# One image's convolution shared between VectorE and TensorE: diagonal taps, a norm by products, and a new pace for the image ahead

## The chip, the cores and the metric

The kernel runs on one core of a Trainium2 chip. Its time is given in device microseconds (us); a figure for a kernel is the median of several executions. One further execution is taken with the hardware profiler, and all rows of the profile come from that one.

## The reference

The input `x` holds 16 images of 56 × 56 tokens with 384 channels, in float32. Two layers follow each other, both with a residual and a group norm of 32 groups (12 channels each) ahead:

```python
# layer 0: windowed attention (windows of 7 x 7, 12 heads of 32, shifted by 3)
x = x + _L0_conv_ref(_gn(x), w_qkv, w_out, b_out, rel_pos_table)
# layer 1: depthwise convolution, 3 x 3, one filter per channel
x = x + _L1_conv_ref(_gn(x), L1_conv_w)

def _gn(v, G=32, eps=1e-5):
    g = v.reshape(B_, H_, W_, G, C_ // G)
    m = jnp.mean(g, axis=(1, 2, 4), keepdims=True)
    s = jnp.var(g, axis=(1, 2, 4), keepdims=True)
    return ((g - m) / jnp.sqrt(s + eps)).reshape(v.shape)

def _L1_conv_ref(x, w):
    w_clip = jnp.clip(w, -1.0, 1.0)
    binary_kernel = w_clip + lax.stop_gradient(jnp.sign(w_clip) - w_clip)
    k = binary_kernel.reshape(kh, kw, 1, C * mult)
    return lax.conv_general_dilated(x, k, ..., padding='SAME', feature_group_count=C)
```

The convolution's weights are the signs of the clipped `w`. The second norm's sums run over a whole image, so no band of an image can be convolved before the attention of its last window is done.

## The kernel before, in words

Channels lie on the partitions: three chunks (`NC`) of 128 channels. The attention works in stripes of 7 rows (8 per image, 128 in all), and each stripe in two units of 4 windows, so there are 256 units, 16 (`NU`) per image. `all_units` walks the units and writes out the order by hand: `heavy(u)` gives the products of a unit (`value`, `query_key`, `project`), and between them stand scores (L458), softmax (L475), exponential (L493), the sums by key (`add_up`, L529), the inverse (L567 to L570, ScalarE and then VectorE), `attend` (L549) and `divide` (L577). `project` (L588) adds the residual on VectorE (L596), takes the second norm's statistics (L602), and sends the stripe through POOL's queue into `mid`, a DRAM tile with the wrap-around columns repeated (L608 to L613).

The convolution of an image runs beside the attention of the next one. `plan_conv` gives each of its steps a due time in units (`at(when, f, ...)`), and `all_units` starts a step when its time comes; the program order on each engine is the order in which the steps are started, and each engine and each DMA queue takes them in that order. An image has 12 pieces: 4 bands (`NB`) of 14 rows (`BR`), each with 3 chunks. For a piece, `band` loads 16 rows from `mid` through SP's queue into one of two buffers `xb` (L636); `pad` has ScalarE write the normalized rows into `hp`, a frame of 16 × 58 with zeros around, of which there are two (L651); `middle` has ScalarE write residual and center tap into `acc` (L663, with the factors that `center` prepared); `tap` has VectorE add the other eight taps, one instruction each (L676). When the three chunks of a band are done, `store` has TensorE transpose them, 112 tokens at a time, into PSUM banks (L687), ScalarE copies them out (L688), and SP stores them (L692), two tiles per store with three buffers. PSUM has four banks for all this (`bank`), taken in turn.

The norm ahead of it is `norm_gather` (means and variances per channel, L244 and L246; then by DMA through DRAM to one group per partition, L248 and L250) and `norm_scale` (folds over the 12 channels of a group on POOL, the power, and by DMA through DRAM back to channels, L285 and L287).

All images have `step` 1.3 units per piece; image 14, which runs beside the attention of image 15, has 1.1, so that its last steps fall behind unit 255:

```python
plan_conv(b - 1, NU * b, 1.3 if b < B - 1 else 1.1, 3, 0.6, nc.gpsimd)
```

Image 15 has no attention to run beside. Its plan has step 1.0 and starts at unit 256; what is left of image 14's plan is sorted in by the due times, and all is started in that order:

```python
plan_conv(B - 1, B * NU, 1.0, 1.3, 0.1, nc.sync)
for _, g, a in sorted((i for u in side for i in side[u]), key=lambda i: i[0]):
    g(*a)
```

After it come a few small steps that test whether a softmax overflowed (L846 to L855); if so, a slower path runs again, which doesn't happen with these inputs. The input `gmat` holds, for each pair of chunks that share a group, a 128 × 128 matrix with 1/12 where two channels are of one group; the kernel before doesn't read it.

Of the kernel before, what the change touches and what calls it, by code (L numbers as in the profile page):

```python
# [9 lines left out]
F32 = mybir.dt.float32  # L10
I32 = mybir.dt.int32
AF = mybir.ActivationFunctionType
# [3 lines left out]
WIN = 7  # L16
SHIFT = WIN // 2
GROUPS = 32
EPS = 1e-5
# [15 lines left out]
def kernel(  # L35
# [57 lines left out]
    def bank(name):  # L93
        return ps.tile([P, 512], F32, tag="mm", name=name)
# [7 lines left out]

    least = const.tile([P, 1], F32, tag="least", name="least")
    reach = const.tile([P, 2, B * NU], F32, tag="reach", name="reach")
    seen = const.tile([P, B], F32, tag="seen", name="seen")
    again = const.tile([P, 1], I32, tag="again", name="again")
    wq_t = const.tile([P, NC, 3 * C], F32, tag="wq", name="wq_t")
    wo_t = const.tile([P, NC, C], F32, tag="wo", name="wo_t")
# [144 lines left out]
    def norm_scale(key, queue, pool=nc.gpsimd):  # L253

        gt = parts.pop(key)
        name = "%d_%d" % key
        g = small.tile([GROUPS, 4], F32, tag="g", name=f"g{name}")
        mean, var, rstd, shift = (g[:, n : n + 1] for n in range(4))
        if key[0]:
            var = seen[:GROUPS, key[1] : key[1] + 1]  # L260
        dev = small.tile([GROUPS, GS], F32, tag="dev", name=f"dev{name}")

        def fold(x):

            n = GS
            while n > 1:
                half = n // 2
                pool.tensor_tensor(x[:, :half], x[:, :half], x[:, n - half : n], ALU.add)
                n -= half

        pool.tensor_copy(dev, gt[:, :, 0])
        fold(dev)
        pool.tensor_scalar(mean, dev[:, 0:1], 1.0 / GS, None, ALU.mult)
        pool.tensor_tensor(dev, gt[:, :, 0], mean.to_broadcast([GROUPS, GS]), ALU.subtract)
        pool.tensor_tensor(dev, dev, dev, ALU.mult)
        pool.tensor_tensor(dev, dev, gt[:, :, 1], ALU.add)
        fold(dev)
        pool.tensor_scalar(var, dev[:, 0:1], 1.0 / GS, EPS, ALU.mult, ALU.add)
        nc.gpsimd.tensor_tensor(rstd, var, power[:GROUPS], ALU.pow)
        pool.tensor_tensor(shift, mean, rstd, ALU.mult)  # L280
        pool.tensor_scalar(shift, shift, -1.0, None, ALU.mult)
        both = small.tile([GROUPS, GS, 2], F32, tag="both", name=f"both{name}")
        pool.tensor_copy(both, g[:, 2:4].unsqueeze(1).to_broadcast([GROUPS, GS, 2]))
        by_channel = dram.tile([C, 2], F32, tag="cod", name=f"cod{name}")
        queue.dma_start(by_channel.rearrange("(g n) k -> g (n k)", n=GS), both.rearrange("g n k -> g (n k)"))  # L285
        coef = small.tile([P, NC, 2], F32, tag="coef", name=f"coef{name}", bufs=4)
        queue.dma_start(coef, by_channel.rearrange("(c p) k -> p c k", p=P))  # L287
        coefs[key] = coef

# [287 lines left out]
    def project(s, m):  # L579

        b, r = divmod(s, NS)
        if (1, b) not in stats:
            stats[1, b] = small.tile([P, NC, NS, 6], F32, tag="st1", name=f"st1_{b}", bufs=1)
        if m == 0:
            ys[s] = ypool.tile([P, NC, WIN, R], F32, tag="y", name=f"y_{s}")
        py = bank(f"py_{s}_{m}")
        for c in range(NC):
            nc.tensor.matmul(  # L588
                py[:, :ST],
                wo_t[:, c, m * P : (m + 1) * P],  # L590
                ots[s][:, c, :],
                start=(c == 0),
                stop=(c == NC - 1),
            )
        view = ys[s][:, m, :, SHIFT:R]
        nc.vector.tensor_tensor(  # L596
            view.rearrange("p r (w c) -> p w r c", c=WIN),
            py[:, :ST].rearrange("p (w r c) -> p w r c", r=WIN, c=WIN),
            xs[s][:, m, :].rearrange("p (w r c) -> p w r c", r=WIN, c=WIN),
            ALU.add,  # L600
        )
        nc.vector.bn_stats(stats[1, b][:, m, r, :], view)  # L602
        if m == NC - 1:
            if b not in mids:
                mids[b] = dram.tile([P, NC, H, R], F32, tag="mid", name=f"mid_{b}")
            del xs[s]
            yt = ys.pop(s)
            nc.gpsimd.tensor_copy(yt[:, :, :, 0:SHIFT], yt[:, :, :, W:R])  # L608
            r0 = r * WIN + SHIFT
            n = min(WIN, H - r0)  # L610
            nc.gpsimd.dma_start(mids[b][:, :, r0 : r0 + n, :], yt[:, :, 0:n, :])
            if n < WIN:
                nc.gpsimd.dma_start(mids[b][:, :, 0 : WIN - n, :], yt[:, :, n:WIN, :])  # L613


    mids, bands, outs, centers = {}, {}, {}, {}

    def center(b):

        coef = coefs[1, b]  # L620
        pool = nc.gpsimd
        cen = small.tile([P, NC, 2], F32, tag="cen", name=f"cen_{b}")
        pool.tensor_tensor(cen[:, :, 0], coef[:, :, 0], bo_sb, ALU.mult)
        pool.tensor_tensor(coef[:, :, 1], coef[:, :, 1], cen[:, :, 0], ALU.add)
# [13 lines left out]

    count, padded = [0], {}

    def pad(b, k, c):

        coef, cen = coefs[1, b], centers[b]
        xb, rows, at, n = bands.pop((b, k, c))
        hp = hps[count[0] % 2]
        count[0] += 1
        if k == 0:
            nc.gpsimd.memset(hp[:, 0, :], 0.0)
        if k == NB - 1:
# [7 lines left out]
        )  # L657
        padded[b, k, c] = (hp, xb)

    def middle(b, k, c):  # L660
        hp, xb = padded[b, k, c]
        acc = opool.tile([P, BR, W], F32, tag="o", name=f"o_{b}_{k}_{c}")
        nc.scalar.activation(  # L663
            acc,
            xb[:, 1 : BR + 1, 0:W],
            AF.Identity,
            bias=centers[b][:, c, 1:2],
            scale=centers[b][:, c, 0:1],
        )
        outs[b, k, c] = acc  # L670
# [6 lines left out]
            acc, hp[:, dy : dy + BR, dx : dx + W], dw_t[:, c, t : t + 1], acc, ALU.mult, ALU.add  # L677
        )

    def store(b, k, g):  # L680
        todo = range(g * LG, min((g + 1) * LG, BR * W // OT))
        flat = [outs[b, k, c].rearrange("p h w -> p (h w)") for c in range(NC)]
        xo = io.tile([P, LG, C], F32, tag="io", name=f"xo_{b}_{k}_{g}")
        for n, t in enumerate(todo):
            po = bank(f"px_{b}_{k}_{t}")
            for c in range(NC):
                nc.tensor.transpose(po[:OT, c * P : (c + 1) * P], flat[c][:, t * OT : (t + 1) * OT], ident)  # L687
            nc.scalar.copy(xo[:OT, n, :], po[:OT, :C])  # L688
        n = len(todo)
        first = k * BR * W + g * LG * OT  # L690
        rows = out[b].rearrange("h w c -> (h w) c")[first : first + n * OT, :]
        nc.sync.dma_start(rows.rearrange("(t p) c -> p t c", p=OT), xo[:OT, :n])  # L692


    side = {}
# [64 lines left out]
    def plan(last_queue):  # L760
        for b in range(1, B):
            plan_load(b)
            plan_conv(b - 1, NU * b, 1.3 if b < B - 1 else 1.1, 3, 0.6, nc.gpsimd)

    def all_units(fast):
        for m in range(2 * NC):
# [12 lines left out]
        for u in range(B * NU):  # L779
# [25 lines left out]
                    g(*a)  # L805
            for _, g, a in light:
                g(*a)
        plan_conv(B - 1, B * NU, 1.0, 1.3, 0.1, nc.sync)
        for _, g, a in sorted((i for u in side for i in side[u]), key=lambda i: i[0]):
            g(*a)  # L810
        side.clear()
# [2 lines left out]
    with tc.manual_schedule():  # L814
# [30 lines left out]
        for n in range(2):  # L845
            nc.vector.tensor_scalar(reach[:, n], reach[:, n], MOST[n], None, ALU.is_lt)  # L846
        nc.vector.tensor_reduce(worst[:, 0:1], reach.rearrange("p n u -> p (n u)"), AX.X, ALU.min)
        fine = small.tile([P, B], F32, tag="fine", name="fine")
        nc.vector.tensor_scalar(fine, seen, 1.0e37, None, ALU.is_lt)
        nc.vector.tensor_reduce(worst[:, 1:2], fine, AX.X, ALU.min)  # L850
        pf = bank("pf")
# [69 lines left out]
```

## Time and profile before

| | us |
|---|---|
| Median of 3 runs | 4300.38 (4299.23 to 4300.46) |
| The profiled execution | 4298.77 |
| Its span, first to last instruction | 4297.0 |
| TensorE busy over the span | 4125.1 (96%) |
| VectorE | 3478.0 (81%) |
| ScalarE | 2479.2 (58%) |
| GpSimd (POOL) | 1800.4 (42%) |
| Granted TensorE clock, mean | 0.980 |

A row of the timeline reads: start in us from the span's start, duration, engine and line, operation, out<-in by the program's names, shapes, how many instructions were merged into the row; in brackets how long the engine had been idle and whose step ended that. PE is TensorE's matmuls, PEld its weight loads, DVE VectorE, ACT ScalarE, SPq the DMA issues of SP's queue. A float32 product shows as two matmuls and two weight loads, a transpose as one of each.

The attention's last product ends at about 4158 us; some 139 us of the span come after it.

### The profile page before, as it was taken

What the parts mean: (1) busy time and instruction counts of PE and PEld (TensorE: products, weight loads), DVE (VectorE), ACT (ScalarE), POOL (GpSimd) and SP (SyncE); (2) the same over time, 40 slices, a digit from 0 to 9 for tenths busy, and PEclk for the clock granted to TensorE, in tenths of its full rate; (3) what the DMA queues carried; (4) which work ended last, traced back from release to release, by engine and by line L of the source; (5) the groups of instructions that cost most, each with busy time, mean ns of one, the idle gap of its engine ahead of it and who ended that gap; (6) DMA issues with size and microseconds to landing.
All of it is one profiled execution on the core that took longest, in us unless ns stands there. A gap on an engine that the chain in (4) does not pass through costs nothing.

```text
span 4297.0 us, 155602 instructions
## 1 busy us (share of the span) xinstructions
PE 4125.1 (96%) x68041; PEld 2628.4 (61%) x68041; DVE 3478.0 (81%) x4387; ACT 2479.2 (58%) x5269; POOL 1800.4 (42%) x3182
## 2 busy tenths in 40 slices
PE   5999999999999999999999999999999999999961
PEld 3666666666666666666666666666666666666641
DVE  4546879788887888888788887878888788887878
ACT  2545656566565656656565665656656565665542
POOL 4453545254443534535345454535444353441000
PEclk8999999999999999999999999999999999999985
DMA  4434445454444544445454444545444454443332
GB/s 90 79 66 82 109 103 123 101 110 110 108 101 109 117 103 114 109 101 112 99 118 107 108 106 104 122 101 109 107 111 100 109 117 102 115 101 87 97 84 88
DMA packets 997170, 444.81 MB, mean 104 GB/s; under 512 B 877690, under 2 KB 935067, under 8 KB 996482
## 3 DMA queue, kind: packets, MB, share of 16 engines
q1 hardware_dynamic: 906480, 272.64, 30.0%
q0 software_dynamic: 87824, 159.76, 15.1%
q8 instruction: 538, 8.81, 0.9%
q10 hardware_dynamic: 2178, 2.38, 0.2%
q14 instruction: 150, 1.23, 0.1%
HBM read 174.86 MB, written 158.47 MB: 78 GB/s over the span
## 4 chain that ended last, share of the span: by engine, by line
PE 94%; DVE 3%; DMA 1%; issue 1%; ACT 0%; SPq 0%; POOL 0%; ACTq 0%; DVEq 0%; POOLq 0%
PE pq L404 36%; PE pv L417 18%; PE py L588 18%; PE ps L458 7%; PE po L549 7%; PE ps L529 4%; PE px L687 3%; DVE o L676 2%; SPq L440 0%; DMA xl<-in_x_dram 0%; DMA wl<-in_L_conv_w_out_dram 0%; DMA xn<-in_x_dram 0%; DMA out_dram<-xo 0%; DMA vq<-in_x_dram 0%; DMA e<-in_x_dram 0%
## 5 line engine op out<-in xcount | busy, mean ns | idle before, releaser
L404 PE MATMUL pq<-xn,wq_t 128*128 128x392 f32 x4608 | 1591.4, 497 | 0.0
L676 DVE SCALAR_TENSOR_TENSOR o<-hp,dw_t,o 128x784 f32<-128x784 f32 x1536 | 1559.4, 1020 | 31.8 <-ACT o L663 17.7
L351 POOL DMA_DIRECT2D xl<-in_x_dram x1980 | 1328.8, 724 | 179.7 <-DVE xt L368 105.1
L404 PEld LDWEIGHTS pq<-xn,wq_t 128*128 128x128 f32 x4608 | 844.6, 188 | 586.8 <-issue 2.6
L588 PE MATMUL py<-ot,wo_t 128*128 128x392 f32 x2304 | 820.2, 498 | 3.9 <-DVE ot L577 3.9
L417 PE MATMUL pv<-xn,wq_t 128*128 128x392 f32 x2304 | 816.8, 496 | 1.3 <-ACT xn L393 1.3
L411 ACT COPY qk<-pq 128x392 f32<-128x392 f32 x768 | 371.4, 484 | 704.6 <-PE pq L404 701.0
L569 DVE SCALAR_TENSOR_TENSOR ln<-ps,inv 128x588 f32<-128x588 f32 x256 | 197.0, 769 | 540.2 <-ACT inv L568 536.5
L608 POOL COPY y<-y 128x63 f32<-128x63 f32 x128 | 33.5, 262 | 1392.3 <-DVE y L596 1392.2
L417 PEld LDWEIGHTS pv<-xn,wq_t 128*128 128x128 f32 x2304 | 420.3, 188 | 284.6 <-ACT xn L393 2.4
L588 PEld LDWEIGHTS py<-ot,wo_t 128*128 128x128 f32 x2304 | 421.5, 190 | 274.4 <-DVE ot L577 4.1
L424 ACT COPY vt<-pv 128x392 f32<-128x392 f32 x384 | 189.2, 493 | 450.7 <-PE pv L417 449.7
L493 ACT ACTIVATE e<-e 128x1176 f32<-128x1176 f32 x256 | 303.1, 1184 | 234.2 <-DVE e L475 234.2
L458 PEld LDWEIGHTS ps<-qk 32*64 32x64 f32 x24576 | 308.5, 131 | 144.5 <-issue 106.0
L549 PE MATMUL po<-e,v 49*32 49x49 f32 x24576 | 363.1, 212 | 8.2 <-DMA v<-vq 7.5
L475 DVE SCALAR_TENSOR_TENSOR e<-ps,bias 128x1176 f32<-128x1176 f32 x256 | 349.2, 1364 | 26.3 <-PE ps L458 24.3
L549 PEld LDWEIGHTS po<-e,v 49*32 49x32 f32 x24576 | 354.1, 105 | 13.9 <-issue 8.8
L458 PE MATMUL ps<-qk 32*64 32x49 f32 x24576 | 340.9, 225 | 1.5 <-issue 1.2
L687 PE MATMUL px<-ident,o 128*112 128x128 f32 x1344 | 202.7, 286 | 103.7 <-DVE o L676 89.7
L380 ACT COPY x<-xt 128x196 f32<-128x196 f32 x720 | 225.8, 369 | 93.8 <-DVE xt L368 92.6
L428 DVE STREAM_TRANSPOSE vq<-vt 128x512 f32<-128x512 f32 x384 | 267.6, 698 | 5.9 <-ACT vt L424 5.7
L688 ACT COPY xo<-px 112x384 f32<-112x384 f32 x448 | 195.1, 482 | 123.7 <-PE px L687 94.1
(120 smaller groups left out, 3653.6 us busy)
## 6 DMA issues: line engine op xcount, KB each, us to landing
v<-vq SPq DMA_DIRECT2D x2048, 48.0 KB
mid<-y POOLq DMA_DIRECT2D x112, 619.5 KB
xl<-in_x_dram POOLq DMA_DIRECT2D x1260, 52.5 KB
out_dram<-xo SPq DMA_DIRECT2D x192, 336.0 KB
xb<-mid SPq DMA_DIRECT2D x96, 472.0 KB
xb<-mid SPq DMA_DIRECT2D x96, 442.5 KB
out_dram<-xo SPq DMA_DIRECT2D x64, 168.0 KB
mid<-y POOLq DMA_DIRECT2D x16, 354.0 KB
```

The lines of the kernel that those rows point to most:

```text
L351: nc.gpsimd.dma_start(xz[i * D + lo : i * D + hi, c, k : k + n, :], flat[token : token + n * (hi - lo)].rearrange("(k t) c -> t k c", k=n) ...
L404: nc.tensor.matmul(pq[:, :ST].rearrange("p (w t) -> p w t", t=T), wq_t[:, c, m * P : (m + 1) * P], xn[:, c, :, :T], start=(c == 0), stop=( ...
L411: nc.scalar.copy(qk[:, m, :ST], pq[:, :ST])
L417: nc.tensor.matmul(pv[:, :ST].rearrange("p (w t) -> p w t", t=T), wq_t[:, c, 2 * C + m * P : 2 * C + (m + 1) * P], xn[:, c, :, :T], start= ...
L428: nc.vector.transpose(vq[:, :, :, m].rearrange("p h n d -> p n h d"), vt[:, m].rearrange("p (n w) (j b) -> p n (w j) b", w=2, b=D),)
L458: nc.tensor.matmul(pp[row * HT : (row + 1) * HT, i, k0 : k0 + T], qk[part, NC * fast + j, q0 : q0 + HT], qk[part, NC * (not fast) + j, q0 ...
L475: nc.vector.scalar_tensor_tensor(e, pp[:, :, : NC * 2 * T].rearrange("q i (n k) -> q i n k", k=T), QSCALE, bias[:, int(s % NS == NS - 1)]. ...
L493: nc.scalar.activation(flat, flat, AF.Exp, accum_out=reach[:, 0, u : u + 1])
L549: nc.tensor.matmul(po[w][i * D : (i + 1) * D, (2 * j + r) * T : (2 * j + r + 1) * T], vs[s][keys, n * 2 + r, h * D : (h + 1) * D], by_head ...
L588: nc.tensor.matmul(py[:, :ST], wo_t[:, c, m * P : (m + 1) * P], ots[s][:, c, :], start=(c == 0), stop=(c == NC - 1),)
L676: nc.vector.scalar_tensor_tensor(acc, hp[:, dy : dy + BR, dx : dx + W], dw_t[:, c, t : t + 1], acc, ALU.mult, ALU.add)
L687: nc.tensor.transpose(po[:OT, c * P : (c + 1) * P], flat[c][:, t * OT : (t + 1) * OT], ident)
```

## The change

Four things are done for the last image, and one for the image ahead of it.

- The norm of image 15 (`norm_late`): the group sums are two sets of seven products with `gmat` instead of DMAs through DRAM and folds on POOL; the power stays on POOL, and `center` runs on VectorE.
- The third chunk of each band (c = 2) of image 15: `convolve` makes its eight outer taps by TensorE, with `hp` as weights (114 columns: two rows of 56 tokens and the two between) and a diagonal matrix per tap as the moving operand; the ninth product adds `acc` by the identity. The result comes out by token, so it needs no transpose; `carry` copies it from PSUM to SBUF (ScalarE) and stores it (SP, two DMAs per band). The other two chunks keep their taps on VectorE, and `store` takes two chunks.
- What this needs is prepared at units 250 to 253.4 (`fetch_late`, `diagonal`), in buffers of the pool that held the stripes' inputs.
- `plan_last` gives all steps of image 15 their due times. `mid`'s last two writes go through SP's queue instead of POOL's.
- Image 14's pace is 0.95 units per piece instead of 1.1.

The diff, without two hunks that only widen the tiles `seen` and `fine` from B to B + NC columns:

```diff
@@ -286,6 +286,66 @@
         coef = small.tile([P, NC, 2], F32, tag="coef", name=f"coef{name}", bufs=4)
         queue.dma_start(coef, by_channel.rearrange("(c p) k -> p c k", p=P))
         coefs[key] = coef
+    late_tiles = {}
+    def fetch_late():
+        pairs = group_blocks(C, GS)
+        gm = xpool.tile([P, NC, ST], F32, tag="x", name="gm").rearrange("p c n -> p (c n)")[:, : len(pairs) * P]
+        gm = gm.rearrange("p (n q) -> p n q", q=P)
+        nc.sync.dma_start(gm, gmat)
+        dg = xpool.tile([P, NC, ST], F32, tag="x", name="dg").rearrange("p c n -> p (c n)")[:, : 9 * P]
+        dg = dg.rearrange("p (t q) -> p t q", q=P)
+        hp = xpool.tile([P, NC, ST], F32, tag="x", name="hp_late").rearrange("p c n -> p (c n)")
+        hp = hp[:, : (BR + 2) * (W + 2)].rearrange("p (h w) -> p h w", w=W + 2)
+        acc = xpool.tile([P, NC, ST], F32, tag="x", name="acc_late").rearrange("p c n -> p (c n)")
+        acc = acc[:, : BR * (W + 2)].rearrange("p (h w) -> p h w", w=W + 2)
+        for t in (hp, acc):
+            nc.gpsimd.memset(t, 0.0)
+        late_tiles.update(gm=gm, dg=dg, hp=hp, acc=acc)
+    def diagonal(t):
+        nc.scalar.activation(late_tiles["dg"][:, t], ident, AF.Identity, scale=dw_t[:, NC - 1, t : t + 1])
+    def norm_late(b):
+        st, gm = stats.pop((1, b)), late_tiles["gm"]
+        mv = small.tile([P, NC, 2], F32, tag="mv", name="mv_late")
+        for c in range(NC):
+            nc.vector.bn_aggr(mv[:, c, :], st[:, c].rearrange("p s k -> p (s k)"))
+        nc.vector.tensor_tensor(mv[:, :, 0], mv[:, :, 0], bo_sb, ALU.add)
+        def group_mean(x, name):
+            pg = bank(name)
+            pairs = group_blocks(C, GS)
+            for m in range(NC):
+                of_m = [n for n, (k, j) in enumerate(pairs) if j == m]
+                for n in of_m:
+                    k = pairs[n][0]
+                    nc.tensor.matmul(
+                        pg[:, 4 * m : 4 * m + 1],
+                        gm[:, n, :],
+                        x[:, k : k + 1],
+                        start=(n == of_m[0]),
+                        stop=(n == of_m[-1]),
+                    )
+            return pg[:, : 4 * NC].rearrange("p (m f) -> p m f", f=4)[:, :, 0]
+        mean = group_mean(mv[:, :, 0], "pg_mean")
+        dev = small.tile([P, 3, NC], F32, tag="dev_late", name="dev_late", bufs=1)
+        nc.vector.tensor_copy(dev[:, 2], mean)
+        nc.vector.tensor_tensor(dev[:, 0], mv[:, :, 0], dev[:, 2], ALU.subtract)
+        nc.vector.tensor_tensor(dev[:, 0], dev[:, 0], dev[:, 0], ALU.mult)
+        nc.vector.tensor_tensor(dev[:, 0], dev[:, 0], mv[:, :, 1], ALU.add)
+        var = seen[:, B : B + NC]
+        nc.vector.tensor_scalar(var, group_mean(dev[:, 0], "pg_var"), EPS, None, ALU.add)
+        nc.gpsimd.tensor_tensor(dev[:, 1], var, power.to_broadcast([P, NC]), ALU.pow)
+        coef = small.tile([P, NC, 2], F32, tag="coef", name="coef_late", bufs=4)
+        nc.vector.tensor_copy(coef[:, :, 0], dev[:, 1])
+        nc.vector.scalar_tensor_tensor(coef[:, :, 1], dev[:, 2], -1.0, dev[:, 1], ALU.mult, ALU.mult)
+        coefs[1, b] = coef
...
@@ -608,17 +668,17 @@
             nc.gpsimd.tensor_copy(yt[:, :, :, 0:SHIFT], yt[:, :, :, W:R])
             r0 = r * WIN + SHIFT
             n = min(WIN, H - r0)
-            nc.gpsimd.dma_start(mids[b][:, :, r0 : r0 + n, :], yt[:, :, 0:n, :])
+            queue = nc.sync if s == B * NS - 1 else nc.gpsimd
+            queue.dma_start(mids[b][:, :, r0 : r0 + n, :], yt[:, :, 0:n, :])
             if n < WIN:
-                nc.gpsimd.dma_start(mids[b][:, :, 0 : WIN - n, :], yt[:, :, n:WIN, :])
+                queue.dma_start(mids[b][:, :, 0 : WIN - n, :], yt[:, :, n:WIN, :])
     mids, bands, outs, centers = {}, {}, {}, {}
-    def center(b):
+    def center(b, pool=nc.gpsimd):
         coef = coefs[1, b]
-        pool = nc.gpsimd
         cen = small.tile([P, NC, 2], F32, tag="cen", name=f"cen_{b}")
         pool.tensor_tensor(cen[:, :, 0], coef[:, :, 0], bo_sb, ALU.mult)
         pool.tensor_tensor(coef[:, :, 1], coef[:, :, 1], cen[:, :, 0], ALU.add)
...
@@ -638,12 +698,12 @@
     count, padded = [0], {}
-    def pad(b, k, c):
+    def pad(b, k, c, late=False):
         coef, cen = coefs[1, b], centers[b]
         xb, rows, at, n = bands.pop((b, k, c))
-        hp = hps[count[0] % 2]
-        count[0] += 1
+        hp = late_tiles["hp"] if late else hps[count[0] % 2]
+        count[0] += not late
         if k == 0:
             nc.gpsimd.memset(hp[:, 0, :], 0.0)
         if k == NB - 1:
...
@@ -657,11 +717,11 @@
         )
         padded[b, k, c] = (hp, xb)
-    def middle(b, k, c):
+    def middle(b, k, c, late=False):
         hp, xb = padded[b, k, c]
-        acc = opool.tile([P, BR, W], F32, tag="o", name=f"o_{b}_{k}_{c}")
+        acc = late_tiles["acc"] if late else opool.tile([P, BR, W], F32, tag="o", name=f"o_{b}_{k}_{c}")
         nc.scalar.activation(
-            acc,
+            acc[:, :, :W],
             xb[:, 1 : BR + 1, 0:W],
             AF.Identity,
             bias=centers[b][:, c, 1:2],
...
@@ -677,19 +737,81 @@
             acc, hp[:, dy : dy + BR, dx : dx + W], dw_t[:, c, t : t + 1], acc, ALU.mult, ALU.add
         )
-    def store(b, k, g):
+    def store(b, k, g, chunks=NC):
         todo = range(g * LG, min((g + 1) * LG, BR * W // OT))
-        flat = [outs[b, k, c].rearrange("p h w -> p (h w)") for c in range(NC)]
+        flat = [outs[b, k, c].rearrange("p h w -> p (h w)") for c in range(chunks)]
         xo = io.tile([P, LG, C], F32, tag="io", name=f"xo_{b}_{k}_{g}")
         for n, t in enumerate(todo):
             po = bank(f"px_{b}_{k}_{t}")
-            for c in range(NC):
+            for c in range(chunks):
                 nc.tensor.transpose(po[:OT, c * P : (c + 1) * P], flat[c][:, t * OT : (t + 1) * OT], ident)
-            nc.scalar.copy(xo[:OT, n, :], po[:OT, :C])
+            nc.scalar.copy(xo[:OT, n, : chunks * P], po[:OT, : chunks * P])
         n = len(todo)
         first = k * BR * W + g * LG * OT
-        rows = out[b].rearrange("h w c -> (h w) c")[first : first + n * OT, :]
-        nc.sync.dma_start(rows.rearrange("(t p) c -> p t c", p=OT), xo[:OT, :n])
+        rows = out[b].rearrange("h w c -> (h w) c")[first : first + n * OT, : chunks * P]
+        nc.sync.dma_start(rows.rearrange("(t p) c -> p t c", p=OT), xo[:OT, :n, : chunks * P])
+    summed = {}
+    def convolve(b, k, c):
+        hp, _ = padded[b, k, c]
+        pitch = W + 2
+        both = pitch + W
+        hp, acc = (a.rearrange("p h w -> p (h w)") for a in (hp, outs[b, k, c]))
+        tiles = BR * W // OT
+        summed[k] = []
+        for first in range(0, tiles, 4):
+            n = min(4, tiles - first)
+            pc = bank(f"pc_{k}_{first}")
+            summed[k].append((first, n, pc))
+            for i in range(n):
+                here = pc[:both, i * P : (i + 1) * P]
+                row = 2 * (first + i)
+                for t in (0, 1, 2, 3, 5, 6, 7, 8):
+                    dy, dx = divmod(t, 3)
+                    nc.tensor.matmul(
+                        here,
+                        hp[:, (row + dy) * pitch + dx : (row + dy) * pitch + dx + both],
+                        late_tiles["dg"][:, t],
+                        start=(t == 0),
+                        stop=False,
+                    )
+                nc.tensor.matmul(here, acc[:, row * pitch : row * pitch + both], ident, start=False, stop=True)
+    def carry(b, k, c):
+        by_token = xpool.tile([P, NC, ST], F32, tag="x", name=f"xc_{k}").rearrange("p c n -> p (c n)")
+        tiles = BR * W // OT
+        both = 2 * W + 2
+        for first, n, pc in summed.pop(k):
+            nc.scalar.copy(by_token[:both, first * P : (first + n) * P], pc[:both, : n * P])
+        rows = out[b].rearrange("h w c -> (h w) c")[k * BR * W : (k + 1) * BR * W, c * P : (c + 1) * P]
+        for j in range(2):
+            nc.sync.dma_start(
+                rows.rearrange("(t j p) c -> j p t c", j=2, p=W)[j],
+                by_token[j * (W + 2) : j * (W + 2) + W, : tiles * P].rearrange("p (t c) -> p t c", c=P),
+            )
+    def plan_last(b, first):
+        at(first, norm_late, b)
+        at(first + 0.1, center, b, nc.vector)
+        for k in range(NB):
+            for c in (2, 0, 1):
+                n = 2 * k + c
+                when = first + 0.5 + (2 * k if c == 2 else n)
+                at(when - (0.1 if c == 2 else 0.2), band, b, k, c)
+                at(when - (0.05 if c == 2 else 0.15), pad, b, k, c, c == 2)
+                at(when - (0.04 if c == 2 else 0.14), middle, b, k, c, c == 2)
+                if c == 2:
+                    at(when + 0.2, convolve, b, k, c)
+                    at(when + 1.3, carry, b, k, c)
+                    continue
+                for i, t in enumerate((0, 1, 2, 3, 5, 6, 7, 8)):
+                    at(when + i / 8, tap, b, k, c, t)
+            for g in range(-(-BR * W // OT // LG)):
+                at(first + 0.5 + 2 * k + 2.02 + 0.01 * g, store, b, k, g, NC - 1)
     side = {}
...
@@ -760,7 +882,10 @@
     def plan(last_queue):
         for b in range(1, B):
             plan_load(b)
-            plan_conv(b - 1, NU * b, 1.3 if b < B - 1 else 1.1, 3, 0.6, nc.gpsimd)
+            plan_conv(b - 1, NU * b, 1.3 if b < B - 1 else 0.95, 3, 0.6, nc.gpsimd)
+        at(B * NU - 6, fetch_late)
+        for t in range(9):
+            at(B * NU - 5 + 0.3 * t, diagonal, t)
     def all_units(fast):
         for m in range(2 * NC):
...
@@ -805,7 +930,7 @@
                     g(*a)
             for _, g, a in light:
                 g(*a)
-        plan_conv(B - 1, B * NU, 1.0, 1.3, 0.1, nc.sync)
+        plan_last(B - 1, B * NU)
         for _, g, a in sorted((i for u in side for i in side[u]), key=lambda i: i[0]):
             g(*a)
         side.clear()
```

## The prediction

> **What bounds the kernel now.** I read the chain that ended last first, limited to the last 167 us, because the diff touches only image 14's convolution (its pace) and everything of image 15 after its attention:
>
> ```profile
> by line: DVE o L676 60.0%; issue 10.0%; PE py L588 4.1%; DMA mvd<-mv 2.3%; DMA out_dram<-xo 1.6%; DMA gt<-mvd 1.6%; DMA coef<-cod 1.2%; ACT xo L688 1.1%; PE px L687 1.1%; DVE st L602 1.0%; POOL dev L268 0.9%; DVE ln L570 0.9%; DVE ln L569 0
> ```
>
> Before this stretch TensorE is busy without a gap; here VectorE's taps (L676) carry the end. The timeline gives the three stages I price: last unit, norm, convolution.
>
> ```profile
> 4141.00 1.38 DVE L475 SCALAR_TENSOR_TENSOR e<-ps,bias 128x1176 f32<-128x1176 f32 x1
> 4142.29 5.37 DVE L676 SCALAR_TENSOR_TENSOR o<-hp,dw_t,o 128x784 f32<-128x784 f32 x5
> 4143.59 1.03 ACT L663 ACTIVATE o<-xb,cen 128x784 f32<-128x784 f32 x1
> ...
> 4147.58 0.76 DVE L569 SCALAR_TENSOR_TENSOR ln<-ps,inv 128x588 f32<-128x588 f32 x1
> ...
> 4161.52 0.82 DVE L244 BATCH_NORM_AGGREGATE mv<-st 128x2 f32<-128x48 f32 x3
> ...
> 4178.31 1.09 ACT L651 ACTIVATE hp<-xb,coef 128x840 f32<-128x840 f32 x1 [31.07 <-POOL coef L624]
> ...
> 4181.19 101.59 DVE L676 SCALAR_TENSOR_TENSOR o<-hp,dw_t,o 128x784 f32<-128x784 f32 x96 [17.71 <-ACT o L663]
> ```
>
> Image 14's taps stand between the last softmax and the last product; from the statistics' end (4161.52) to the first padded band (4178.31) 16.8 us pass; then 96 taps run in 101.59 us, 1.058 each, nearly without a gap. Two more things matter, TensorE's transposes at both clocks and how long a band takes to come:
>
> ```profile
> 4124.33 0.82 PE L687 MATMUL px<-ident,o 128*112 128x128 f32 x6
> 4206.66 4.30 PE L687 MATMUL px<-ident,o 128*112 128x128 f32 x19 [7.98 <-DVE o L676]
> 4261.12 0.41 SPq L636 DMA_DIRECT2D xb<-mid  x1
> 4266.41 1.09 ACT L651 ACTIVATE hp<-xb,coef 128x840 f32<-128x840 f32 x1 [3.69 <-DMA xb<-mid]
> ```
>
> In the trace the first six start 108 ns apart (clock 1.00), the nineteen 213 ns apart (clock 0.50). A band costs 4.2 us (4187.56 to 4191.72) to 5.3 us (these rows) from issue to pad. The table of TensorE's clock by window:
>
> ```profile
> 4147.40:4150.80 3.40, 0.72 (x1) 0.50 0.00 0
> 4150.80:4154.20 3.40, 3.40 (x7) 0.50 0.00 0
> 4154.20:4157.70 3.50, 3.50 (x12) 1.00 0.00 0
> 4157.70:4161.10 3.40, 0.83 (x4) 0.99 0.00 0
> 4161.10:4164.50 3.40, 0.96 (x5) 0.50 0.64 190
> 4232.70:4236.10 3.40, 3.40 (x17) 0.50 0.34 101
> 4236.10:4239.50 3.40, 0.18 (x1) 0.99 0.88 248
> ```
>
> (us, busy us, granted clock): one filled window of 3.4 us raises the clock, an idle one or two drop it.
>
> **What the Trainium skill says.** "TensorE: Matmul & The Clock Gate", Part 1 (The HAM clock gate): cold is half rate, and a busy window of some 3.4 us lifts it; the table above agrees. Same page, Architectural detail: ScalarE and VectorE take instructions strictly in order, and TensorE only pulls weight loads ahead. The trace agrees for weights: the load for L588 at 4124.87 (190 ns) overlaps the last px transpose, and its matmul starts 108 ns after that load began. Part 4 says that transposes don't lift the clock; here they do (4232.70 window: transposes only, then 0.99). "DMA: Bandwidth & Descriptors", Anatomy of one DMA, puts about 2 us of fixed cost on a transfer; here 3 KB takes 1.3 to 3.8 us in the chain (cod, mvd).
>
> **The change, part by part.** Times count from the moment the last image's coefficients are ready, 4178.31 before.
>
> *A. Image 14 at pace 0.95.* Its last tap moves from unit 256.06 to 254.28, its last store from 257.7 to 255.9: both leave the tail. In the units before, taps rise from some 14.5 us in 32 (two units) by 1.1/0.95 to 16.8; with the other 11.5 us VectorE stands at 28.3 of 32, as it does in the two units from 3774 (28.25, TensorE 32.00), so nothing there; without that cover it would cost about 1 us a unit. In the last unit, the softmax (4141.00, scores done 4138.35) comes 2.7 us earlier without the three taps ahead of it, and L569 0.9 earlier without the five (L568 ended by 4146.6); the ACT row at 4143.59 goes too, but TensorE was late there, not ScalarE. So the division is 3.6 us earlier; the last statistics no longer wait for a tap (0.9), nor does L244 (0.8); six of image 14's px now stand between the products (+0.6). Sum −4.7 us; ends −3 (more px in the way) and −8 (the products all warm). Moved with it: mid's last two writes go from POOL's queue to SP's, behind y's copy and ahead of the last store; the band that needs them is due only 10 us later. Also added: a 458 KB load on SP at unit 250 (0.35 us of SP, some 1.5 us of DMA under v's loads, needed a unit later), two memsets on a POOL that is idle there, nine diagonals on ScalarE (below L380's 0.37 us each, at 58% busy): nothing, at most 1 us if v is late.
>
> *B. The norm.* Off: four small DMAs and some twenty POOL steps, 16.8 us. On: aggregates 1.0; seven products twice, each two passes with one moving column. No such row; the nearest is L852 (two loads 0.22 apart at half clock), so 14 × 0.11 to 0.22 = 1.5 to 3.0, plus 0.7 start and read-out: 2.7 (still warm) and 3.5. Four VectorE steps 0.9, one 0.3, the power on POOL 0.57 (L279) with hand-offs 0.8, two steps 0.4, center's first two 0.5, hand-offs 0.1: 10.2. −6.6 us, ends −4 and −9.
>
> *C. The convolution.* Off VectorE: 32 taps, 33.9 us. On TensorE: per band 7 tiles × 9 products × 2 passes (as L404 has two records per product) of 128 columns against 114 weight columns = 126 passes. No row has it; the px pass has its columns and nearly its weights, and L588's load its kind. At 0.1085 a pass it is 13.7 us, at 0.213 26.8. TensorE is idle ahead of each band, so it starts cold; some 4.4 us pass until a filled window ends (20.6 passes), the rest is warm: 15.9, or 15.6 where transposes run just before.
>
> Now the order. All queues are in program order, and SP issues band (k+1,0) after band k's two carry stores, which wait for ScalarE's copies, which wait for convolve k; on ScalarE the pad of (k+1,0) is behind those copies too. So from E, the end of convolve k: last copy 0.8 (L688 0.48 and the hop); two stores of 392 pieces at 0.66 (v<-vq, eight of 384 pieces in 5.27 us) and a hop 1.4; band's landing 4.6; pad and middle 2.1: **taps (k+1,0) start at E+8.9.** Pad and middle of the third chunk +2.0 (E+10.9); only then do the copies of store k run, which free the banks that convolve k+1 stands behind on TensorE, +1.7 (E+12.6); convolve 15.6: **next E at E+28.2**, against 16.9 of VectorE's work per band.
>
> First E: pads and middle 3.1 + 15.9 = 19.0. Third E: 19.0 + 56.4 = 75.4; taps (3,0) start 84.3. Band (3,1) is issued behind store 2, whose fourth copy waits for a buffer of the first to land: 86.3 + 0.8 + 2.4 + 1.2 = 90.7; landing 4.2, pad and middle 2.1; taps (3,1) from 97.0 to 105.5. Convolve 3 ends at 103.6. Before: last tap at 4282.78 − 4178.31 = 104.5. So VectorE's saved 33.9 us come back as idle: +1.0. The last store has seven 256-column copies and fewer transposes: 4.3 us instead of 5.0 (4282.83 to 4287.79), −0.7. Sum +0.3.
>
> Total −4.7 − 6.6 + 0.3 = −11.0 us: span 4286.0 from 4297.0, or 4287.8 from the profiled execution's 4298.77; the median of the runs lies 1.6 higher, so 4300.4 − 11.0 = 4289.4. About 0.2% (8.6 us) can be told from no change; this is 0.26%.
>
> **Rivals.**
> *VectorE stays the bound* (or the loop is shorter). For it: TensorE's warm work (4 × 13.7) is below VectorE's 64 × 1.058 = 67.7 us. Then the last tap is at 69.8, −35.4 for C, 4253.7. Against it: band and pad stand behind the carry in two queues. With convolve warm throughout (13.7) and bands at 3.3 the loop is 25.0, C −11.5: 4277.6.
> *TensorE cold: slower.* If the clock stays at 0.50 through a band, convolve is 26.8, the loop 39.4, the fourth E 148.1: +42.8 on the end of the taps, 4332. For it: TensorE is idle some 10 us ahead of each band, and the px burst from 4206.66, which filled no window, didn't lift the clock. Against it: the L588 run did after 4.1 us, and convolve fills several windows. It decides from 18.8 us a band (149 ns a pass: 3.2 us more each makes up the 11), also if a weight load held the array for its whole 190 ns.
> *Hand-offs eat the rest.* Bands at 5.3 and slower issue give a loop of 31, three times +2.9: 4298, no change to be told.
>
> **How the numbers follow.** The walk as computed 0.58 (own range 4283 to 4296: loop ±1.7 three times, A and B ±2), of it 0.42 beyond 8.6 us and 0.16 within; shorter loop 0.15, all faster; cold TensorE 0.15, slower; hand-offs 0.12, 0.10 within and 0.02 slower. Faster 0.57, same 0.26, slower 0.17. The range 4262 to 4314 leaves out about half of the two outer cases.
>
> **What would show it.** Right: 64 taps in some 103 us with gaps of 7 to 10 us ended by ScalarE's middle ahead of (k+1,0) and 4 us ahead of (k+1,1); SP's carry waits on ScalarE, ScalarE's on TensorE; convolve bursts of 15 to 16 us, one per 28 us, first 4 us at 0.50; L244's successor to first pad 10 us; no L676 in the last unit. Wrong: taps without gaps; a burst under 13 or over 19 us; TensorE waiting for VectorE in units 243 to 254; a first pad that waits for its band.

## The result, and the profile after

The changed kernel takes 4287.47 us (median of 11 runs, 4284.65 to 4291.69) against 4299.23 of the kernel before (11 runs): a ratio of 0.9974, 95% interval 0.9965 to 0.9983, or some 11 to 12 us less. The prediction said 4289.4, counted from a median of 4300.4; from 4299.23 its −11.0 would be 4288.2. The profiled execution has a span of 4287.3 us.

The sum is right; its terms are not all right. Cut at the four places that the prediction used, the two profiled executions compare so:

| stretch, us | before | after | change | predicted |
|---|---|---|---|---|
| start to the last image's aggregates (A) | 4161.52 | 4163.18 | +1.7 | −4.7 |
| aggregates to the first pad (B) | 16.80 | 8.80 | −8.0 | −6.6 |
| first pad to the last tap (C) | 104.47 | 104.47 | 0.0 | +1.0 |
| last tap to the end (C's tail) | 14.20 | 10.80 | −3.4 | −0.7 |
| sum | 4297.0 | 4287.3 | −9.7 | −11.0 |

The +1.7 in A is not the work of the edits. At the softmax of unit 243, where image 14's pieces begin, the profile of the changed kernel is already 2.0 us later (3952.95 instead of 3950.97), and a second profile of it is 3.1 us earlier than the first (3949.87). From that softmax to the aggregates the changed kernel takes 210.2 us, the kernel before 210.6. What the pace does there is taken up below, over all profiles.

The timeline of the changed kernel, with the rows that answer to those shown of the kernel before (L736 are the taps, L535 the softmax, L317 the aggregates, L711 pads, L723 middles):

```profile
4143.94 3.17 DVE L736 SCALAR_TENSOR_TENSOR o<-hp,dw_t,o 128x784 f32<-128x784 f32 x3
4147.03 1.38 DVE L535 SCALAR_TENSOR_TENSOR e<-ps,bias 128x1176 f32<-128x1176 f32 x1
...
4163.18 0.81 DVE L317 BATCH_NORM_AGGREGATE mv_late<-st 128x2 f32<-128x48 f32 x3
...
4164.34 1.69 PE L327 MATMUL pg_mean<-mv_late,gm 128*128 128x1 f32 x14 [1.95 <-DVE mv_late L318]
...
4166.97 3.06 PE L327 MATMUL pg_var<-dev_late,gm 128*128 128x1 f32 x14 [0.94 <-DVE dev_late L341]
...
4170.32 0.90 POOL L344 TENSOR_TENSOR dev_late<-seen,power 128x3 f32<-128x3 f32 x1 [7.35 <-DVE seen L343]
...
4171.98 1.09 ACT L711 ACTIVATE hp<-xb,coef_late 128x840 f32<-128x840 f32 x1 [9.08 <-DVE coef_late L684]
```

Three taps of image 14 still stand ahead of the last softmax. The norm's fourteen passes cost 1.69 us with the clock up (1.00 granted from 4164.30 to 4166.00) and 3.06 with it down (0.51 from 4166.97 to 4170.05).

The convolution's first turn, from the same timeline of the changed kernel (L773 and L780 are convolve's products, L788 carry's copies, L791 its stores, L696 the bands' loads, L748 the copies of `store`):

```profile
4175.09 3.73 PE L773 MATMUL pc<-dg,hp_late 128*114 128x128 f32 x16 [5.05 <-issue]
...
4181.81 1.91 PE L773 MATMUL pc<-dg,hp_late 128*114 128x128 f32 x16
...
4191.41 0.38 PE L780 MATMUL pc<-ident,acc_late 128*114 128x128 f32 x2
...
4191.83 0.48 ACT L788 COPY xc<-pc 114x384 f32<-114x384 f32 x1 [5.31 <-PE pc L780]
4192.34 0.84 SPq L791 DMA_DIRECT2D out_dram<-xc  x2
...
4193.34 0.83 SPq L696 DMA_DIRECT2D xb<-mid  x2
4197.60 1.14 ACT L711 ACTIVATE hp<-xb,coef_late 128x896 f32<-128x896 f32 x1 [5.29 <-DMA xb<-mid]
4198.65 1.03 ACT L723 ACTIVATE o<-xb,cen 128x784 f32<-128x784 f32 x1
...
4199.71 8.53 DVE L736 SCALAR_TENSOR_TENSOR o<-hp,dw_t,o 128x784 f32<-128x784 f32 x8 [8.62 <-ACT o L723]
...
4201.55 1.91 ACT L748 COPY xo<-px 112x256 f32<-112x256 f32 x6
...
4203.27 3.62 PE L773 MATMUL pc<-dg,hp_late 128*114 128x128 f32 x16
```

This is the loop of the prediction, row by row: convolve ends, its last copy runs on ScalarE, the two stores are issued on SP, only then the next band's load, it lands, pad and middle, and VectorE, idle for 8.62 us, starts its next taps. The four convolves start at 4175.09, 4203.27, 4232.08 and 4259.72: 28.2, 28.8 and 27.6 us apart, against 16.9 of VectorE's work.

The waits of the changed kernel over its last stretch (engine, line, what it waited for, us in total, times, longest) show where the 34 us went that VectorE no longer computes:

```profile
DVE o L736 <- ACT o L723: 35.8, 7, 8.6
ACT hp L711 <- DMA xb<-mid: 33.0, 7, 6.4
ACT xc L788 <- PE pc L780: 32.0, 8, 6.3
```

### The profile page after: what moved, and what is told of

Same layout as the page of the kernel before. It is cut to its first block, busy times and chain, and to the rows that moved or that the text cites. A ratio compares the mean times of both kernels' runs of the same rounds, so it can differ in the third digit from the quotient of the medians.

```text
span 4287.3 us, 156586 instructions
## 1 busy us (share of the span) xinstructions
PE 4182.8 (98%) x68545; PEld 2688.1 (63%) x68545; DVE 3448.4 (80%) x4367; ACT 2482.8 (58%) x5286; POOL 1796.1 (42%) x3160
## 5 line engine op out<-in xcount | busy, mean ns | idle before, releaser
L736 DVE SCALAR_TENSOR_TENSOR o<-hp,dw_t,o 128x784 f32<-128x784 f32 x1504 | 1527.5, 1020 | 49.1 <-ACT o L723 35.8
L535 DVE SCALAR_TENSOR_TENSOR e<-ps,bias 128x1176 f32<-128x1176 f32 x256 | 349.2, 1364 | 25.9 <-PE ps L518 24.7
L609 PEld LDWEIGHTS po<-e,v 49*32 49x32 f32 x24576 | 354.6, 105 | 14.2 <-issue 8.3
L656 DVE TENSOR_TENSOR y<-py,x 128x392 f32<-128x392 f32 x384 | 215.1, 560 | 62.7 <-PE py L648 57.5
L453 ACT ACTIVATE xn<-x,coef 128x392 f32<-128x392 f32 x384 | 247.2, 713 | 13.9 <-DVE dwl L182 13.9
```

Of the source, the lines that this page charges most:

```text
L453: nc.scalar.activation(xn[:, c, :, :T], xs[s][:, c, :].rearrange("p (w t) -> p w t", t=T), AF.Identity, bias=coef[:, c, 1:2], scale=coef[: ...
L535: nc.vector.scalar_tensor_tensor(e, pp[:, :, : NC * 2 * T].rearrange("q i (n k) -> q i n k", k=T), QSCALE, bias[:, int(s % NS == NS - 1)]. ...
L609: nc.tensor.matmul(po[w][i * D : (i + 1) * D, (2 * j + r) * T : (2 * j + r + 1) * T], vs[s][keys, n * 2 + r, h * D : (h + 1) * D], by_head ...
L736: nc.vector.scalar_tensor_tensor(acc, hp[:, dy : dy + BR, dx : dx + W], dw_t[:, c, t : t + 1], acc, ALU.mult, ALU.add)
```

## Experiments on the pace and the norm

These four ran on one chip; the kernel before stood at 4298.48 us there.

**The changed kernel again.**

> The changed kernel once more, beside the three others on the same chip: 0.997 of the kernel before, some 11 to 12 us less.

Measured: 4287.73 us, ratio 0.9975 (0.9966 to 0.9984). It is the base for what follows.

**Pace 0.95 alone, in the kernel before.**

```diff
-            plan_conv(b - 1, NU * b, 1.3 if b < B - 1 else 1.1, 3, 0.6, nc.gpsimd)
+            plan_conv(b - 1, NU * b, 1.3 if b < B - 1 else 0.95, 3, 0.6, nc.gpsimd)
```

> The kernel before with image 14's pace 0.95 and nothing else. Step A as predicted: 4.7 us less, about 4294.5. By the changed kernel's trace: 0 to 1 us less (TensorE gives back in units 243 to 254 what the last unit gains), 4298 to 4299.5; the scores of unit 255 should start some 4 us later than before, and the first pad of image 15 at about the same time.

Measured: 4298.49 us, ratio 1.0002 (0.9993 to 1.0010). The pace by itself is worth nothing that can be told. Its profile has the scores' softmax of unit 255 at 4144.32 instead of 4141.00, and the aggregates at 4162.20 instead of 4161.52. The waits of TensorE in that profile, from the softmax of unit 243 to just behind that of unit 255 (3951 to 4147 us):

```profile
PE ps L458 <- DVE ln L569: 2.6, 1, 2.6
PE px L687 <- DVE o L676: 2.3, 1, 2.3
PE pq L404 <- ACT ot L559: 0.2, 1, 0.2
```

From the softmax of unit 243 to that of 255 it takes 193.3 us instead of 190.0 (193.7 and 194.1 in two profiles of the changed kernel). 2.8 of the 3.3 are there by unit 254's softmax: five more of `store`'s tiles have been transposed by then (28 instead of 23 copies of them). These 15 px are all that TensorE has more to do up to there (2951 matmuls instead of 2936); its busy time is 2.6 us longer (180.3 instead of 177.7), and it waits for 0.2. Between the softmaxes of units 254 and 255 stand 2 px instead of the 15 of the kernel before. But the scores of unit 255 now wait 2.6 us for VectorE's L569 (0.3 before), so the stretch that lost these transposes gets no shorter (12.8 us instead of 12.3). What the last unit gains is 2.6 us (17.9 us from its softmax to the aggregates instead of 20.5). The two nearly cancel. The other profiles agree: from unit 243's softmax to the aggregates, the three kernels with pace 1.1 (before, and the two runs that follow) take 210.5 to 210.6 us each, the seven profiles with pace 0.95 take 210.2 to 212.4, four of them more than 211.4. The pace, with what else differs in six of these kernels, costs there about a microsecond or nothing.

**Pace back at 1.1, in the changed kernel.**

```diff
-            plan_conv(b - 1, NU * b, 1.3 if b < B - 1 else 0.95, 3, 0.6, nc.gpsimd)
+            plan_conv(b - 1, NU * b, 1.3 if b < B - 1 else 1.1, 3, 0.6, nc.gpsimd)
```

> The changed kernel with image 14's pace set back from 0.95 to 1.1; all else stays. Step A as predicted (the pace is worth 4.7 us): about 4292, 4.7 above the changed kernel. What the changed kernel's trace shows (the units from 243 on run 4 us late, and the three taps still stand ahead of the last softmax): the pace is worth nothing by itself, but image 14's last store would come back into the tail, ahead of the pad of piece (0,1) on ScalarE and behind the first convolution on TensorE, which costs some 3 to 5 us there: 4287 to 4290. If the pace only costs, 4283.

Measured: 4301.23 us, ratio 1.0004 (0.9996 to 1.0013): 13.5 us slower than the changed kernel, so the whole gain is gone. All three numbers expected were misses; the direction of the second was right and its size far too small. The first pad comes at nearly the same time as in the changed kernel (4171.54 and 4171.98), but the last tap 117.1 us after it instead of 104.5. The timeline of this run shows why:

```profile
4190.85 0.82 PE L747 MATMUL px<-ident,o 128*112 128x128 f32 x6
4191.38 0.86 ACT L748 COPY xo<-px 112x384 f32<-112x384 f32 x2 [15.90 <-PE px L747]
...
4193.80 0.43 SPq L696 DMA_DIRECT2D xb<-mid  x1
4198.23 1.09 ACT L711 ACTIVATE hp<-xb,coef_late 128x840 f32<-128x840 f32 x1 [4.88 <-DMA xb<-mid]
...
4200.35 8.53 DVE L736 SCALAR_TENSOR_TENSOR o<-hp,dw_t,o 128x784 f32<-128x784 f32 x8 [18.16 <-ACT o L723]
...
4202.01 0.97 ACT L788 COPY xc<-pc 114x512 f32<-114x512 f32 x2
```

Image 14's last store is left over for the tail. Its transposes stand behind the first convolve on TensorE, its copies on ScalarE wait 15.90 us for them, and behind these copies and stores stand the load and the pad of piece (0,1): VectorE idles 18.16 us, and carry's copies, at 4202.01, are 10 us later than in the changed kernel (4191.83). The pace is thus not a saving but what keeps this store out of the queues of the new plan.

**The norm by products alone, in the kernel before.**

```diff
-        at(first, norm_gather, (1, p), queue)
-        at(first + 0.1, norm_scale, (1, p), queue)
-        at(first + 0.2, center, p)
+        if p == B - 1:
+            at(first, norm_late, p)
+            at(first + 0.1, center, p, nc.vector)
+        else:
+            at(first, norm_gather, (1, p), queue)
+            at(first + 0.1, norm_scale, (1, p), queue)
+            at(first + 0.2, center, p)
...
+        at(B * NU - 6, fetch_late)
```

> The kernel before with the last image's norm by products, and nothing else. Step B as predicted: 6.6 us less, 4292.6; as the changed kernel's trace has it (8.8 us from the aggregates to the first pad instead of 16.8): 8 us less, 4291.2, perhaps 1 us more because one tap of image 14 falls between the norm's steps. A rival, that the first band's load takes the norm's place as the last to come: under 3 us less.

Measured: 4293.24 us, ratio 0.9988 (0.9981 to 0.9995), 5.2 us less: short of both numbers expected, and more than the 3 us of the rival. In its profile the aggregates lie 11.1 us ahead of the first pad, 5.7 less than before: both rounds of products run at the low clock (3.12 us each), and a tap of image 14 stands between the coefficients and `center`. The same stretch takes 8.8 us in the changed kernel, so 2.3 us of B's 8.0 come from the other edits: no tap is left over, and the products of the last unit have kept the clock up for the first round (1.69 us). Most of it comes with the pace: the run before, the changed kernel with pace 1.1, takes 10.7 us for the stretch, with the tap left over and 2.71 us for the first round.

## Experiments on the convolution's order

These four ran on another chip, with the kernel before at 4298.44 us there. The changed kernel was not run beside them; it is taken at the 4287.73 us of the runs above, where the kernel before stood within 0.1 us of this.

**Loads ahead of the carry.** In `plan_last`:

```diff
-                at(when - (0.1 if c == 2 else 0.2), band, b, k, c)
+                at(first + 2 * k - (0.29 if c == 2 else 0.3) if k and c != 1 else when - (0.1 if c == 2 else 0.2), band, b, k, c)
```

> The changed kernel with one thing moved: the loads of pieces (k+1,0) and (k+1,2) stand ahead of band k's carry on SP's queue, so that they come while convolve k runs; ScalarE's order stays. If SP's order is a part of the loop (E to E 28 us), the carry's issue and the landing, some 6 us, leave it: loop 22, last tap some 17 us earlier, about 4271. If VectorE or TensorE alone sets the pace, or ScalarE's order, no change: 4287.

Measured: 4270.26 us, ratio 0.9932 (0.9915 to 0.9948), 17 us less than the changed kernel. Only SP's order is different. In the profile the last tap comes 83.0 us after the first pad, 21.5 less than in the changed kernel; the walk had some 17. That the totals agree so well is in part chance, for the aggregates come 2.4 us later in this profile (4165.61) than in that of the changed kernel, in a stretch that the edit doesn't touch.

**Pad and middle of (k+1,0) ahead of the carry too,** on top of the edit above:

```diff
+                early = 0.57 if k and c == 0 else 0.0
-                at(when - (0.05 if c == 2 else 0.15), pad, b, k, c, c == 2)
-                at(when - (0.04 if c == 2 else 0.14), middle, b, k, c, c == 2)
+                at(when - (0.05 if c == 2 else 0.15) - early, pad, b, k, c, c == 2)
+                at(when - (0.04 if c == 2 else 0.14) - early, middle, b, k, c, c == 2)
```

> As the run with the bands first, and ScalarE's pad and middle of piece (k+1,0) also stand ahead of band k's carry. VectorE then doesn't wait for convolve k: taps (1,0) follow (0,1) at once; left are the waits for piece (k,1), whose load stands behind the stores, and the third chunk's pad behind the carry. Walked in the same way: last tap 80 us after the first pad instead of 104, about 4263. If ScalarE's order costs nothing by itself: as the run with the bands first, 4271.

Measured: 4265.11 us, ratio 0.9920 (0.9903 to 0.9936). The last tap comes 80.0 us after the first pad, as walked (83.0 in the run before). That this is below the run before it can't be told from the two intervals alone, but the timeline's tap rows can: here 24 taps run without a gap, in the run before 16. The run before, from its first tap row to its last (three rows left out), and then this run:

```profile
4176.04 16.97 DVE L736 SCALAR_TENSOR_TENSOR o<-hp,dw_t,o 128x784 f32<-128x784 f32 x16 [1.75 <-ACT o L723]
4195.09 8.53 DVE L736 SCALAR_TENSOR_TENSOR o<-hp,dw_t,o 128x784 f32<-128x784 f32 x8 [2.08 <-ACT o L723]
...
4248.34 8.60 DVE L736 SCALAR_TENSOR_TENSOR o<-hp,dw_t,o 128x784 f32<-128x784 f32 x8 [2.93 <-ACT o L723]
```

```profile
4174.03 25.41 DVE L736 SCALAR_TENSOR_TENSOR o<-hp,dw_t,o 128x784 f32<-128x784 f32 x24 [1.75 <-ACT o L723]
4204.35 16.97 DVE L736 SCALAR_TENSOR_TENSOR o<-hp,dw_t,o 128x784 f32<-128x784 f32 x16 [4.91 <-ACT o L723]
4224.34 17.04 DVE L736 SCALAR_TENSOR_TENSOR o<-hp,dw_t,o 128x784 f32<-128x784 f32 x16 [3.02 <-ACT o L723]
4243.31 8.60 DVE L736 SCALAR_TENSOR_TENSOR o<-hp,dw_t,o 128x784 f32<-128x784 f32 x8 [1.93 <-ACT o L723]
```

**The third chunk's pad ahead of the carry as well, and the load of piece (k+1,1) ahead of the stores,** with a second pair of frames for the third chunk:

```diff
-        hp = late_tiles["hp"] if late else hps[count[0] % 2]
+        hp = late_tiles["hp", k % 2] if late else hps[count[0] % 2]
...
+            start = t - 0.3 if k else t + 0.3
+            at(start, band, b, k, 0)
+            at(start + 0.01, band, b, k, 2)
+            at(start + 0.02, pad, b, k, 0)
+            at(start + 0.03, middle, b, k, 0)
+            at(start + 0.04, pad, b, k, 2, True)
+            at(start + 0.05, middle, b, k, 2, True)
+            at(t + 1.85, carry, b, k, 2)
+            at(start + 0.18, band, b, k, 1)
+            at(start + 0.25, convolve, b, k, 2)
+            at(t + 1.35, pad, b, k, 1)
+            at(t + 1.36, middle, b, k, 1)
...
+                at(t + (1.89 if k < NB - 1 else 2.52) + 0.01 * g, store, b, k, g, NC - 1)
```

(`t` is `first + 2 * k`; `acc` gets its second frame like `hp`; the taps' due times lie closer together so that `store` may follow at `t + 1.89`. By these due times the loads and pads of pieces (k+1,0) and (k+1,2) stand ahead of band k's carry; the load of piece (k+1,1) stands behind the carry and ahead of band k's stores, its pad behind their copies.)

> All loads and pads of band k+1 ahead of band k's carry: two pairs of frames for the third chunk, so that its pad doesn't wait for convolve k, and piece (k,1)'s load ahead of the stores. Then a band costs the longer of VectorE's 16.9 us and TensorE's convolve with the transposes, some 17: last tap 70 to 73 us after the first pad, about 4254. If something else holds the bands apart (the stores' buffers, the clock), 4262 and more.

Measured: 4260.20 us, ratio 0.9912 (0.9895 to 0.9928), 38 us below the kernel before and 27 below the changed one. This version beats both. Its last tap comes 72.7 us after the first pad; convolve takes 15.4, 13.7, 13.9 and 13.7 us, since TensorE rests for at most 2.4 us at a time between bands and the clock stays up. The median is above what was expected; the profiled span is 4255.1. Its timeline has VectorE's taps nearly closed:

```profile
4173.71 25.41 DVE L738 SCALAR_TENSOR_TENSOR o<-hp,dw_t,o 128x784 f32<-128x784 f32 x24 [1.75 <-ACT o L725]
4200.31 16.97 DVE L738 SCALAR_TENSOR_TENSOR o<-hp,dw_t,o 128x784 f32<-128x784 f32 x16 [1.19 <-ACT o L725]
4217.43 17.04 DVE L738 SCALAR_TENSOR_TENSOR o<-hp,dw_t,o 128x784 f32<-128x784 f32 x16
4235.71 8.60 DVE L738 SCALAR_TENSOR_TENSOR o<-hp,dw_t,o 128x784 f32<-128x784 f32 x8 [1.24 <-ACT o L725]
```

**Fewer products.** `convolve` with two of its eight taps:

```diff
-                for t in (0, 1, 2, 3, 5, 6, 7, 8):
+                for t in (0, 1):
```

> The changed kernel with the taps 2 to 8 left out of the last image's third chunk on TensorE (two taps and the identity stay, 42 passes for a band instead of 126); VectorE's work and all orders stay. If convolve's length is on the loop, a band gets 9 us shorter until VectorE's taps and the loads take over: last tap some 78 us after the first pad, about 4262. If convolve is hidden beside VectorE, no change: 4287.

Measured: 4266.54 us, ratio 0.9925 (0.9906 to 0.9945), 21 us less than the changed kernel, with six products a tile left out. Last tap 80.0 us after the first pad. Convolve's length lies on the path; cutting it to a third gives about as much as the second of the three reorderings (4265.11), and they leave no work out.

## Why the prediction was right, and where it wasn't

**C, the loop: right by its mechanism and nearly by its size.** From the ends of the first three convolves (4191.8, 4219.5, 4247.6) the taps of the next band's first piece start at +7.9, +9.0 and +8.6 (predicted +8.9), ScalarE comes to `store`'s copies at +9.8, +10.9 and +10.4 (+10.9), and the next convolve starts at +11.5, +12.6 and +12.2 (+12.6). From end to end a turn takes 27.7, 28.1 and 27.5 us (28.2). Convolve takes 16.4, 16.0, 15.2 and 15.1 us from the start of its first pass to that of its last (15.9, then 15.6): one pass is 0.109 us warm (sixteen take 1.91 with the last one's end) and 0.213 cold, and by these two figures some 14 to 27 passes at the start run cold. The carry's two stores were over-priced, 0.82 to 0.84 us instead of 1.3; the load behind them took 4.3 to 5.5 us to the pad instead of 4.6. That the loop is made of SP's and ScalarE's orders and of convolve's length is shown by taking each out: the last tap, 104.5 us after the first pad in the changed kernel, comes at 83.0 with SP's order changed alone (the walk's 17 us less would be some 88), at 80 with ScalarE's too (80), at 73 with the rest (70 to 73), and at 80 with the short convolve (78). The rival that VectorE stays the bound falls for the change as it is, and nearly comes true once the orders are changed: 4260 against the rival's 4254. The cold rival falls on the pass times.

**A, the pace: wrong.** The step that failed is "the softmax (4141.00, scores done 4138.35) comes 2.7 us earlier without the three taps ahead of it". Taps due at 254.04 to 254.28 are started in unit 254 ahead of the step that starts unit 255's softmax, so three taps are there again, in the row at 4143.94. The second fault is the "nothing there" for the units before: VectorE's mean load was right (27 to 29 of 32 us) and TensorE was busy nearly without a gap, but 15 transposes moved ahead of unit 254's softmax and took 2.6 us of TensorE, and the wait of the next scores for VectorE ate what their leaving had freed: +3.3 us. The prediction had named TensorE waiting for VectorE in units 243 to 254 as a sign against itself. From the softmax of unit 243 to the aggregates the pace is worth nothing or costs a microsecond, instead of −4.7; alone it changes the kernel's time by nothing that can be told (ratio 0.9993 to 1.0010).

**What the pace does instead** has no price in the prediction: without it the new plan is 13.5 us slower. The prediction does say that image 14's last store leaves the tail, and its walk of C has no such store in it, but it credits the pace with the −4.7 in A alone. In the plan of before the late store costs little; in the new one a queue of products and a carry stand ahead of it and the pad of (0,1) behind it.

**B, the norm: right, a little more than said.** 8.0 instead of 6.6. From the end of one VectorE step to the start of the next, the first products took 1.9 instead of 2.7 and the second 3.25 instead of 3.5. The power with its hand-offs took 1.0 instead of 0.8 (L344 itself 0.90 instead of 0.57; the prediction's terms add up to its 10.2 if the 0.8 includes the 0.57). The small steps took 2.65 in all instead of 3.2. 5.7 of the 8.0 is the norm's own, as the run with the norm alone shows.

**C's tail: mis-sized, −3.4 instead of −0.7.** Seen in the rows after the last tap, of the kernel before and then of the changed one:

```profile
4282.83 4.30 PE L687 MATMUL px<-ident,o 128*112 128x128 f32 x19 [8.04 <-DVE o L676]
...
4286.93 0.43 PE L852 MATMUL pf<-worst,ones 128*128 128x2 f32 x2
```

```profile
4276.51 1.81 PE L747 MATMUL px<-ident,o 128*112 128x128 f32 x13 [1.35 <-DVE o L736]
...
4278.16 0.38 PE L977 MATMUL pf<-worst,ones 128*128 128x2 f32 x2
```

Convolve has left the clock up (1.00 granted from 4276.50 to 4278.30, against 0.50 from 4282.83 to 4286.90 before), so 13 transposes take 1.81 us where 19 took 4.30, and the product of the final test, which stands behind them on TensorE, starts 1.7 us after the last tap instead of 4.1. The prediction had followed the stores only. The profiles speak for the test and against the stores. Here are the last copy out of PSUM and the test's last step, of the kernel before and then of the run with the loads moved ahead, whose last tap ends at 4256.94:

```profile
4287.29 0.48 ACT L688 COPY xo<-px 112x384 f32<-112x384 f32 x1 [0.28 <-DMA out_dram<-xo]
4287.59 0.15 DVE L855 TENSOR_SCALAR again<-both_fine 128x1 int32<-128x1 f32 x1
```

```profile
4259.27 0.15 DVE L980 TENSOR_SCALAR again<-both_fine 128x1 int32<-128x1 f32 x1
...
4261.60 0.37 ACT L748 COPY xo<-px 112x256 f32<-112x256 f32 x1 [2.45 <-DMA out_dram<-xo]
```

The last copy ends 5.0 us after the last tap in both; the test ends 5.0 us after it in the kernel before and 2.5 in the other run, and the span ends 14.2 and 11.6 us after it. The end went with the test. No run changed the test's chain alone, and the rest of the 3.4 can't be told: over the ten profiles the span ends 7.9 to 9.6 us after the test's last step.

So the errors, +6.4 in A and −1.4, −1.0 and −2.7 in the others, cancel to 1.3 in the span. That the total was met is luck in this: A gave nothing, the tail gave more than was said, and 2.0 of A's 6.4 stood in that one profile before the pace could act.

## What to carry to other kernels

When work is moved to another engine, walk one turn of the loop through every queue it now passes, DMA issues included: here the moved third was paid back to the last microsecond by a load standing behind a store in one queue and a pad behind a copy in another, and 27 us came free by due times and a second pair of frames alone. Price an edit against the schedule that it will run in: a pace worth nothing in the old plan was worth 13.5 us in the new one. And check in which unit a step is started, not only when it is due.

## What the runs showed of the hardware

A row of transposes alone lifts TensorE's clock (before, 4232.70 to 4236.10 filled at 0.50, 0.99 after). The clock can be carried from one stage to the next: convolve costs 15.1 to 16.4 us in the changed kernel, where TensorE has rested 5 to 10 us shortly ahead of it, and 13.7 to 13.9 in the last reordering, where only 2 to 6 us, with transposes in them, lie between two convolves. Where the one turns into the other was not found: with the loads alone moved ahead, some 6 us lie between two convolves, and the later ones took 14.4 to 16.0. Fourteen passes with a single moving column and 128 columns of weights cost 1.69 us at the high clock and 3.06 to 3.12 at the low one, 0.12 and 0.22 each: about as much as a pass with 128 moving columns, 0.109 and 0.213, so a narrow moving operand saved nothing here.
